# Row sums of the first triangle stage on ScalarE, low parts of two batches made one stage later, and a new order of words

## The chip, the cores and the metric

The kernel runs on one core of a Trainium2 chip. The metric is the device time of one execution in microseconds (us). Before the change three runs took 3619.18, 3623.9 and 3624.72 us; the median is 3623.9.

## What is computed

The input is x, four batches of 64 x 64 positions with 256 channels, in float32. Two layers follow each other. The first is an attention over the 4096 positions of a batch with 32 channels for its factors f and g:

```
f = xt @ Wf + bf;  g = xt @ Wg + bg;  v = xt @ Wh + bh
beta = softmax(einsum('bqd,bkd->bqk', g, f))
x = x + (einsum('bqk,bkd->bqd', beta, v) @ Wo + bo)
```

The second is a triangle attention over the 64 x 64 positions with 8 heads, layer norms and an MLP:

```
scores = einsum('bilhd,bljhd->biljh', q, k) / sqrt(32)
att = softmax(scores, axis=2)                       # over l
out = einsum('biljh,bilhd,bljhd->bijhd', att, v1, v2)
h = layer_norm(x_in + out @ Wo)
x = layer_norm(relu(h @ W1 + b1) @ W2 + b2 + h)
```

The change touches the softmax sums over l of the triangle attention of batch 0, and the factors f and g of the attention of batches 2 and 3.

## The kernel before, in words

A batch goes through a token stage (`layer0`, the first attention and the projections of the second layer) and a triangle stage (`first_layer1` for batch 0, `next_layer1` for the others). Token stages and triangle stages follow each other; all that batch 0's triangle stage has to spare is used to make the inputs of batches 1, 2 and 3. Each engine works its own queue in order, and all queues are filled in the order of the program.

**The triangle stage.** It has 32 steps: four pairs of heads by eight groups of eight rows i (`NIG`, `IG`). What a step needs is made in pieces that words name:

- `sp`, `sf`: the score matmuls for a pair (L940), into a tile of the PSUM pool psA, which has two buffers and also holds the accumulators; `e`, `f`: ScalarE's exponentials of them into the SBUF tile S (L950).
- `S`: for one step, VectorE sums the 8 rows of 64 exponentials into `dens` (L967) and takes the reciprocal (L969). `W`: ScalarE multiplies each row by its reciprocal (L977). `t`: TensorE turns the result into the PSUM tile att (L994). `c`: ScalarE copies the last two or three of its eight pieces to the SBUF tile attP (L1002)[...].
- `R`: one of the eight products of a step with v2, 128 x 2048 float32 (L1042). The last `npool(step)` of the eight are made by GpSimd from attP into tile Rp (two buffers), the others by VectorE from att into tile R (three buffers). In batch 0 `npool` is 3, and 2 in every fourth step.
- `V`: ScalarE writes the stationary weights wsel from v1 (L1021). `A`: TensorE accumulates one product (L1052). `T`: ScalarE takes one of the two accumulators of a step to SBUF (L1062), and after the second the step's eight stores go out on SP's queue (L1071).

In the triangle stage of batch 0 other words stand between these. For piece s (512 tokens; pieces 0 to 7 are batch 1, 8 to 15 batch 2, 16 to 23 batch 3), class `Ahead` makes the inputs of a later token stage: `v` the value matmuls from tile xT (L383), `u` their copy out (L390); `g` the matmuls of g and f into a PSUM tile of the pool psB (L251), `a` ScalarE's copy of them with bias, rounded to the number format of the score matmuls, the high part (L260), `b` VectorE's low part, the sum with bias less the high part (L265), and the store of both to DRAM (L273). A copy of the high and low parts is spread later to the tiles gT and fT by DMAs on GpSimd's queue (L278, L284). When both `v` and `g` of piece s are done, the load of the xT of piece s + 2 is issued on SP's queue (L377). The words `m`, `n`, `o`, `p` are projections of batch 0 that are left over from its token stage (L481, L443).

**The order.** `ORDER0` is a list of words that is gone through once for each of 11 periods. A period is four steps; the word `R25/2` stands for product 5 of step 4i + 2, and the number after the slash is i's lag: i is the period less 2. A word whose step or piece doesn't exist does nothing; words of step 0 for `S`, `W`, `V`, `t` and `c` do nothing either, since `layer0` has done them. Periods with i from 0 to 3 handle two pieces s each, and periods with i from 4 to 7 four.

**The token stage.** `layer0` runs over g = 0 to 63, eight groups for each of eight query blocks. For each g, TensorE makes four score matmuls (L563) and four value matmuls (L590), ScalarE two exponentials (L575), VectorE an addition to the running sum (L597). After each group a piece of the query block before is done (`parts`): the normalisation, the output and the projections, whose results go to DRAM on SP's queue. Nothing of `Ahead` is in the token stage of batch 1.

Of the kernel before, what the change touches and what calls it, by code (L numbers as in the profile page):

```python
# [25 lines left out]
IG = 8  # L26
NIG = N // IG
# [37 lines left out]


ORDER0 = """
    A21/2 g1/2 S3/1 W1/1 A27/2 A23/2 A26/2 a1/2 V3/2 A24/2 R32/2 b1/2 m1/2 T20/2 c3/2 t0/1 v2/2 n1/2 R25/2 A25/2
    R33/2 sp0/1 T21/2 A32/2 R34/2 R36/2 R30/2 A33/2 e00/1 u2/2 e01/1 o1/2 R31/2 g2/2 c0/1 R37/2 A34/2 A36/2
    A30/2 A31/2 A37/2 V0/1 R35/2 T30/2 t1/1 R00/1 p1/2 a2/2 b2/2 A35/2 R03/1 T31/2 sf0/1 A00/1 R02/1 g0/1 f0/1  # L70
    a0/1 b0/1 R05/1 f1/1 R07/1 A05/1 A03/1 v3/2 R06/1 u3/2 m0/1 S2/1 W2/1 c1/1 v0/1 V1/1 R01/1 A02/1 n0/1 R04/1
    A07/1 A01/1 A04/1 R12/1 u0/1 A06/1 T00/1 sp1/1 T01/1 R13/1 R15/1 R14/1 A13/1 e10/1 e11/1 t2/1 R10/1 A12/1
    R17/1 V2/1 A15/1 A14/1 A10/1 R16/1 R11/1 S0 R22/1 W3/1 g3/2 c2/1 W0 A17/1 R27/1 A11/1 v1/1 R20/1 a3/2 b3/2
    u1/1 o0/1 p0/1 S1 R21/1 T10/1 t3/1 A16/1 T11/1 A20/1 R23/1 A22/1 R24/1 R26/1
""".split()


@with_exitstack
def attention_then_triangle_kernel(
# [174 lines left out]
                    )  # L254


    def biased(ps, t):
        ps = ps.rearrange("p (w t) -> p w t", w=4)
        for w, bias in enumerate((bias_g, bias_f)):
            nc.scalar.activation(t[:, 0, w, :].bitcast(PART), ps[:, w, :], AF.Identity, bias=bias)  # L260

    def parted(ps, t):
        ps = ps.rearrange("p (w t) -> p w t", w=4)
# [5 lines left out]
    def parts_tile(**where):  # L269
        return work.tile([P, 2, 2, P], F32, name="gf", **where)  # L270

    def store_parts(d, q, t, queue):
        queue.dma_start(out=d[q], in_=t)  # L273
# [68 lines left out]
    class Ahead:  # L342
        def __init__(self):
            shapes = {"x": [C, T], "v": [P, NKC, P], "gf": [8, P, 2, 2, P]}
            self.d = {
                b: {n: dram.tile(sh, F32, tag="ah" + n, name="ah" + n, bufs=NB) for n, sh in shapes.items()}
                for b in range(1, NB)
            }
            self.n = 8 * (NB - 1)
            self.raw, self.xT, self.vp, self.gf, self.t = {}, {}, {}, {}, {}  # L350
            self.parts = None

        def bring(self, s):
# [43 lines left out]
        def factored(self, s):  # L397
            if self.parts is None:
                self.parts = work.tile([P, 2, 2, 2, P], F32, tag="hid", name="gf", bufs=1)
            self.t[s] = self.parts[:, s % 2]  # L400
            biased(self.gf[s], self.t[s])

        def parted(self, s):
            t = self.t.pop(s)
            parted(self.gf.pop(s), t)
            store_parts(self.d[1 + s // 8]["gf"], s % 8, t, nc.sync)


# [99 lines left out]
    def layer0(b, F, safe, rest, ahead):  # L508
# [257 lines left out]
        for g in range(8 * NQB):  # L766
            qb, k = divmod(g, 8)
            if b == 0 and not safe:
                for load in later[3 * g : 3 * g + 3]:
                    load()  # L770
                if g == 6:
                    fold_bias()
                if g == 20:
                    add_b2()
            if safe and k == 0 and qb + 1 < NQB:
                mx, todo = pieces(qb + 1)
                for qc, t in todo:
                    max_piece(qc, t, mx)
                row[qb + 1] = max_row(mx)
            values(g, g + 1 < 8 * NQB)  # L780

            if qb > 0 and not (qb == last and k >= 6 + late):
                for part in parts[k]:
                    part(qb - 1)
            if late and g % 2 == 0 and 0 <= g // 2 - 2 < ahead.n:
                ahead.bring(g // 2 - 2)
            if late and g % 2 == 1 and 0 <= g // 2 - 3 < ahead.n:
                ahead.turn(g // 2 - 3)
            for do, after in (
                (rest.recall, -3), (rest.settle, 0), (rest.rooted, 1), (rest.polished, 2), (rest.scaled, 3), (rest.finish, 4),  # L790
            ):
                if b > 1 and g - after in SETTLED:
                    do(NP * (b - 2) + SETTLED.index(g - after))
            if g == 1 and b > 0 and not safe:
                limits(b - 1)
            if qb == last and k == 3:
                L.fetch_v1(0)
                L.fetch_v1(1)
            if qb == last and k == 5:
                if b > 0:  # L800
                    rest.load(NP * (b - 1))
                L.fetch_qk(0, True)
# [81 lines left out]
    class Layer1:  # L884
        def __init__(self, b, io, safe):
            self.b, self.io, self.safe = b, io, safe

            self.aT = dram.tile([C, 2, N // 2, N], F32, tag="aT", name="aT")
            io["a"] = self.aT
            self.S, self.v2, self.qk, self.v1, self.att, self.ao = {}, {}, {}, {}, {}, {}  # L890
            self.R, self.begun, self.acc, self.rec, self.e = {}, {}, {}, {}, {}
            self.owed = lambda: None

# [57 lines left out]
                )  # L953


        def sums(self, step):
            pair, ig = divmod(step, NIG)
            rows = self.S[pair][:, ts(ig, IG), :]
            if self.safe:
                nmx = small.tile([P, IG], F32, tag="mxl", name="mxl")  # L960
                nc.vector.tensor_reduce(nmx, rows, AX.X, ALU.max, negate=True)
                den = small.tile([P, IG], F32, tag="den", name="den")
                for i in range(IG):
                    nc.scalar.activation(rows[:, i, :], rows[:, i, :], AF.Exp, bias=nmx[:, i : i + 1])
            else:
                den = dens[:, ts(step, IG)]
            nc.vector.tensor_reduce(den, rows, AX.X, ALU.add)  # L967
            rec = small.tile([P, IG], F32, tag="rd", name="rd")
            nc.vector.reciprocal(rec, den)  # L969
            self.rec[step] = (rows, rec)  # L970
# [8 lines left out]

        def npool(self, step):  # L980
            if self.b == 0:
                return 2 if step % 4 == 3 else 3
            return 3 - step % 2


# [431 lines left out]
    def step_words(L, fetched, stored, spread, late=None):  # L1417
        made, taken, sps = {}, {}, {}

        def do(w, step, m):  # L1420
            if not 0 <= step < NSTEP:
                return
            if w == "R":
                if step not in made:
                    made[step] = 0
                    L.begin(step)
                L.product(step, m)
                made[step] += 1
                if made[step] == 4:
                    spread(step)  # L1430
                if made[step] == 8:
                    if step == 1:
                        L.fetch_v2(1)
                    if step == NIG - 1 and late is not None:
                        L.fetch_v2(2, 2)
                        late.room = True
                        late.fetch()
                    elif step in (NIG - 1, 2 * NIG - 1):
                        L.fetch_v2((step + 1) // NIG + 1)
                    fetched(step + 1)  # L1440
            elif w == "A":
                L.accumulate(step, m)
            elif w == "T":
                L.take(step, m)
                taken[step] = taken.get(step, 0) + 1
                if taken[step] == 2:
                    L.store(step)
                    stored(step)
            elif step == 0:
                return  # L1450
            elif w == "S":
                L.sums(step)
            elif w == "W":
                L.weights(step)
            elif w == "V":
                L.stationary(step)
                L.fetch_v1(step + 2)
            elif w == "t":
                L.turn_weights(step)
            elif w == "c":  # L1460
                L.copy_weights(step)


        def scores(j):
            if 0 <= j < 12:
                L.scores(1 + j // 4, j % 4)
                sps[j] = L.sp
                if j % 4 == 3 and j // 4 + 2 < NPAIR:
                    L.fetch_qk(j // 4 + 2)

        def take_scores(j, half):
            if 0 <= j < 12:
                L.sp = sps[j]
                L.take_scores(half)

        L.fetch_v1(2)
        return do, scores, take_scores
# [6 lines left out]
    def first_layer1(L, ahead, F):  # L1484
# [29 lines left out]
        for period in range(NSTEP // 4 + 3):  # L1514
            if period == 1:
                L.owed()
            for word, late in words_of(ORDER0):
# [10 lines left out]
                elif word[0] == "f":  # L1528
                    if i == 0:
                        take_scores(0, last)  # L1530
                elif word[0] in "RATSWVtc":
                    step_word(word[0], 4 * i + int(word[1]), last)
                elif word[0] in "mnop":
                    if 0 <= i < 4:
# [199 lines left out]
```

## Time and profile before

One execution was profiled. It took 3623.49 us; the span of the program in it is 3621.6 us, at a mean granted TensorE clock of 0.993.

| | us |
|---|---|
| median of three runs | 3623.9 |
| profiled execution, and its span | 3623.49, 3621.6 |
| TensorE busy over the span | 3516.2 |
| VectorE | 2849.8 |
| ScalarE | 1923.5 |
| GpSimd | 1777.1 |
| first triangle stage, first product to the end of the last | 443.5 to 868.2 |
| first score matmul of the second token stage | 872.2 |

Busy time is the union of an engine's instructions. Matmuls are pipelined and their ends modelled, so a busy TensorE needn't be at its peak. L12 is line 12 of the kernel; PE is TensorE's matmuls, PEld its weight loads, DVE VectorE, ACT ScalarE, POOL GpSimd, SP the queue of most DMAs. The idle time before an instruction is put down to what released it last.

### The profile page before, as it was taken

To read this page: it belongs to the slowest core of one execution; us is meant where nothing else is said; L and a number is where in the kernel's file an instruction comes from. 1 tells how busy PE (TensorE), PEld (TensorE's weight loads), DVE (VectorE), ACT (ScalarE), POOL (GpSimd) and SP (SyncE) were. 2 spreads that over 40 slices of the span, in tenths; PEclk is the share of its full clock that TensorE was granted. 3 is DMA by queue.
4 is the path that set the end of the run, shared out by engine and by line. 5 is a ranking of instruction groups with operands and counts; after the bars stand their busy time and mean duration, and the time that the engine had idled before them with its cause. 6 is when DMAs were issued, how large, how long until landed. Compare 5 with 4: busy or idle time off the path is not lost.

```text
span 3621.6 us, 58681 instructions
## 1 busy us (share of the span) xinstructions
PE 3516.2 (97%) x22218; PEld 1887.8 (52%) x22218; DVE 2849.8 (79%) x2662; ACT 1923.5 (53%) x4221; POOL 1777.1 (49%) x904
## 2 busy tenths in 40 slices
PE   9999999988999999999999999999999999999998
PEld 6555444434555555554455555555355555555477
DVE  4777499996555569999777749999787766999987
ACT  3444455544444366665444446666444446777655
POOL 5000099995000058899111118989611116999920
PEclk9999999999999999999999999999999999999999
DMA  9444555456111264426322254343633335441221
GB/s 174 137 132 125 138 151 133 126 132 139 47 50 50 81 153 102 108 62 114 96 95 88 82 141 117 83 104 79 131 93 99 96 108 142 96 94 49 66 69 57
DMA packets 509492, 374.37 MB, mean 103 GB/s; under 512 B 320080, under 2 KB 450896, under 8 KB 500368
## 3 DMA queue, kind: packets, MB, share of 16 engines
q1 hardware_dynamic: 460160, 343.56, 34.7%
q0 software_dynamic: 36160, 19.94, 5.5%
q10 hardware_dynamic: 12880, 7.01, 0.7%
q8 instruction: 178, 2.92, 0.3%
q14 instruction: 114, 0.93, 0.1%
HBM read 205.73 MB, written 164.63 MB: 102 GB/s over the span
## 4 chain that ended last, share of the span: by engine, by line
PE 68%; POOL 7%; DVE 6%; issue 4%; ACT 2%; DMA 0%; SPq 0%; ACTq 0%; DVEq 0%; POOLq 0%
PE o L590 18%; PE acc L1052 17%; PE proj L673 6%; POOL Rp L1042 6%; PE s L563 5%; PE mp L1303 5%; PE zp L1323 5%; PE sp L940 3%; DVE R L1042 3%; PE v1p L705 2%; PE hp L1160 2%; PE y L642 1%; PE att L994 1%; PE htp L1270 1%; PE hp L1166 0%
## 5 line engine op out<-in xcount | busy, mean ns | idle before, releaser
L1042 POOL TENSOR_TENSOR Rp<-attP,v 128x2048 f32<-128x2048 f32 x328 | 1491.3, 4579 | 410.4 <-ACT attP L1002 367.3
L1042 DVE TENSOR_TENSOR R<-att,v 128x2048 f32<-128x2048 f32 x696 | 1545.9, 2277 | 70.4 <-PE acc L1052 51.8
L590 PE MATMUL o<-e,v 128*128 128x512 f32 x2048 | 1043.7, 592 | 0.0
L575 ACT ACTIVATE e<-s 128x1024 f32<-128x1024 f32 x512 | 522.9, 1023 | 532.4 <-PE s L563 447.6
L597 DVE TENSOR_TENSOR esum<-esum,e 128x2048 f32<-128x2048 f32 x224 | 511.8, 2285 | 369.9 <-ACT e L575 367.9
L563 PE MATMUL s<-gT,fT 128*128 128x512 f32 x1024 | 786.5, 770 | 8.8 <-ACT e L575 4.7
L1052 PE MATMUL acc<-R,wsel 128*32 128x512 f32 x5568 | 705.4, 602 | 27.7 <-DVE R L1042 20.4
L590 PEld LDWEIGHTS o<-e,v 128*128 128x128 f32 x2048 | 388.3, 190 | 276.7 <-issue 233.8
L1062 ACT COPY ao<-acc 128x1024 f32<-128x1024 f32 x256 | 256.3, 1012 | 291.5 <-PE acc L1052 203.3
L1052 PE MATMUL acc<-Rp,wsel 128*32 128x512 f32 x2624 | 345.5, 598 | 22.3 <-POOL Rp L1042 21.6
L1052 PEld LDWEIGHTS acc<-R,wsel 128*32 128x32 f32 x5568 | 155.4, 110 | 397.6 <-issue 277.4
L1337 POOL TENSOR_TENSOR hz<-hz,log_bc 128x512 f32<-128x512 f32 x32 | 45.6, 1426 | 599.9 <-ACT hz L1247 599.9
L563 PEld LDWEIGHTS s<-gT,fT 128*128 128x128 f32 x1024 | 194.4, 190 | 245.0 <-issue 231.9
L977 ACT ACTIVATE es<-S,rd 128x64 f32<-128x64 f32 x1024 | 258.3, 337 | 15.0 <-DVE rd L969 13.1
L1231 POOL TENSOR_SCALAR nt<-mv 128x2 f32<-128x2 f32 (+1 forms) x49 | 9.4, 191 | 505.1 <-DVE mv L1186 500.0
L1303 PE MATMUL mp<-hT,w 128*128 128x256 f32 x1024 | 244.7, 384 | 1.7 <-ACT hT L1275 1.7
L1323 PE MATMUL zp<-w,hid 128*128 128x256 f32 x1024 | 240.0, 385 | 2.5 <-ACT hid L1312 2.1
L1323 PEld LDWEIGHTS zp<-w,hid 128*128 128x128 f32 x1024 | 187.9, 190 | 50.1 <-issue 14.7
L1303 PEld LDWEIGHTS mp<-hT,w 128*128 128x128 f32 x1024 | 185.2, 190 | 54.7 <-ACT attP L1002 12.6
L619 DVE RECIPROCAL rec<-den 128x512 f32<-128x512 f32 x32 | 107.4, 3357 | 126.5 <-PE den L615 121.2
L1052 PEld LDWEIGHTS acc<-Rp,wsel 128*32 128x32 f32 x2624 | 80.9, 110 | 210.1 <-issue 143.6
L950 ACT ACTIVATE S<-sp 128x512 f32<-128x512 f32 x128 | 131.4, 1092 | 77.9 <-PE sp L940 77.9
(195 smaller groups left out, 3699.0 us busy)
## 6 DMA issues: line engine op xcount, KB each, us to landing
v<-v2d SPq DMA_DIRECT2D x44, 512.0 KB
v1c<-v1d SPq DMA_DIRECT2D x128, 128.0 KB
aT<-ao SPq DMA_DIRECT2D x1024, 16.0 KB
A<-aT SPq DMA_DIRECT2D x256, 64.0 KB
hz<-raw SPq DMA_DIRECT2D x32, 512.0 KB
y<-yT SPq DMA_DIRECT2D x56, 256.0 KB
q<-st SPq DMA_DIRECT2D x56, 256.0 KB
k<-st SPq DMA_DIRECT2D x52, 256.0 KB
```

The source lines that it names most:

```text
L563: nc.tensor.matmul(s_ps[r // 2][:, r % 2, :], fT[tt][:, ts(r * 4 + n, P)], gT[qb // 4][:, ts(qb % 4, QB)], start=True, stop=not safe,)
L575: nc.scalar.activation(e[g][:, 2 * j : 2 * j + 2, :], s_ps[j], AF.Exp)
L590: nc.tensor.matmul(o_ps[qb], F.v[tt][:, r * 4 + n, :], es[:, r, :], start=(k == 0 and r == 0), stop=(k == 7 and r == 3),)
L597: nc.vector.tensor_tensor(esum[qb], esum[qb], es, ALU.add)
L673: nc.tensor.matmul(ps, w[:, cc, rows], y(qb, cc), start=(cc == 0), stop=(cc == 1))
L950: nc.scalar.activation(self.S[pair][:, :, l0 : l0 + 8].rearrange("p i l -> p l i"), sp[:, lh], AF.Copy if self.safe else AF.Exp,)
L977: nc.scalar.mul(e[:, i, :], rows[:, i, :], rec[:, i : i + 1])
L1042: eng.tensor_tensor(R, src.unsqueeze(1).to_broadcast([P, D, N]), v2[h], ALU.mult)
L1052: nc.tensor.matmul(acc[32 * c : 32 * c + 32, n % 2, :], w[:, n, c, 16 * h : 16 * h + 32], R[:, ts(c, 8), :].rearrange("p d j -> p (d j)"), ...
L1062: nc.scalar.copy(self.ao[step][:, ts(np, 2)].rearrange("p k d j -> p k (d j)"), self.acc[step][np])
L1303: nc.tensor.matmul(self.mp[:, fc % 2, :], w1_sb[:, cc, ts(fc, P)], self.hT[tt][:, cc, :], start=(cc == 0), stop=(cc == 1),)
L1323: nc.tensor.matmul(zp[:, n, :], self.hid[tt][:, fc, ts(n, P)], w2_sb[:, fc, :], start=(fc == 0), stop=(fc == 3 and tt not in self.hT2),)
```

## The change

1. A new word `K` for each step of the first triangle stage. `row_sums` has ScalarE pass over each of the step's 8 rows with Identity, writing the row onto itself, and take the sum of the row into `dens` with the accumulator output. `sums` then leaves out VectorE's reduce for that step and keeps the reciprocal. Step 0 is summed by VectorE as before.
2. For pieces 8 to 23 (batches 2 and 3) `biased` writes g and f with bias unrounded, and `parted` issues only the store of that, half as large. In the second token stage, `bring_whole` loads such a piece back (for g = 10, 13, ... 55), and two to three rounds later (g = 15, 18, ... 60) `part` has ScalarE make the rounded high part and VectorE the low part, and stores both. The tile has the tag s4, of which there are two buffers. Pieces 0 to 7 stay as they were.
3. `npool` in batch 0 is read from a list of 32 digits, `ON_POOL`; they sum to 83.
4. `ORDER0` is a new list. Its lags differ too: no word has the lag 0 any more, and products 1, 3, 5 and 7 of step 4i + 1 and all of step 4i + 2 have the lag 2.

```diff
 ORDER0 = """
...
+    S3/2 A14/2 R17/2 t2/2 e11/2 o0/2 A12/2 b0/2 K0/1 c2/2 V2/2 R13/2 v2/2 R11/2 R15/2 A17/2 R27/2 W3/2 S0/1
+    A10/2 A13/2 R22/2 R23/2 u2/2 p0/2 A15/2 A11/2 v1/2 T10/2 A22/2 T11/2 A27/2 A23/2 t3/2 m1/2 R21/2 u1/2 R26/2
+    A21/2 R24/2 g1/2 A26/2 A24/2 K1/1 g2/2 c3/2 W0/1 R20/2 A20/2 R25/2 A25/2 n1/2 t0/1 o1/2 a1/2 a2/2 T20/2
+    R32/2 b2/2 v3/2 V3/2 A32/2 V0/1 R37/2 T21/2 A37/2 R35/2 R36/2 R30/2 p1/2 A30/2 c0/1 R34/2 u3/2 A35/2 v0/1
+    A34/2 R31/2 A36/2 K2/1 R33/2 R05/1 sf0/1 T31/2 A31/2 u0/1 R07/1 A33/2 b1/2 S1/1 sp0/1 R04/1 g3/2 T30/2 W1/1
+    e01/1 A05/1 R06/1 A04/1 R03/1 R01/1 e00/1 t1/1 V1/1 f0/1 m0/1 c1/1 A07/1 f1/1 A01/1 K3/1 R00/1 S2/1 A03/1
+    R02/1 g0/1 A06/1 R14/1 A00/1 A02/1 W2/1 R12/1 R10/1 T01/1 a0/1 sp1/1 T00/1 a3/2 R16/1 n0/1 A16/1 b3/2 e10/1
 """.split()
+
+ON_POOL = "23323323233233323233323223322332"
...
-    def biased(ps, t):
+    def biased(ps, t, whole=False):
         ps = ps.rearrange("p (w t) -> p w t", w=4)
         for w, bias in enumerate((bias_g, bias_f)):
-            nc.scalar.activation(t[:, 0, w, :].bitcast(PART), ps[:, w, :], AF.Identity, bias=bias)
+            o = t[:, 0, w, :]
+            nc.scalar.activation(o if whole else o.bitcast(PART), ps[:, w, :], AF.Identity, bias=bias)
...
-            biased(self.gf[s], self.t[s])
+            biased(self.gf[s], self.t[s], whole=s >= 8)
...
         def parted(self, s):
-            t = self.t.pop(s)
-            parted(self.gf.pop(s), t)
+            t, gf, d = self.t.pop(s), self.gf.pop(s), self.d[1 + s // 8]["gf"]
+            if s < 8:
+                parted(gf, t)
+                store_parts(d, s % 8, t, nc.sync)
+            else:
+                nc.sync.dma_start(out=d[s % 8][:, 0], in_=t[:, 0])
+
+        def bring_whole(self, s):
+            t = self.whole[s] = parts_tile(tag="s4")
+            nc.sync.dma_start(out=t[:, 1], in_=self.d[1 + s // 8]["gf"][s % 8][:, 0])
+
+        def part(self, s):
+            t = self.whole.pop(s)
+            nc.scalar.activation(t[:, 0].bitcast(PART), t[:, 1], AF.Identity)
+            nc.vector.tensor_tensor(t[:, 1].bitcast(PART), t[:, 1], t[:, 0], ALU.subtract)
             store_parts(self.d[1 + s // 8]["gf"], s % 8, t, nc.sync)
...
+            if b == 1 and g % 3 == 1 and 8 <= g // 3 + 5 < ahead.n:
+                ahead.bring_whole(g // 3 + 5)
+            if b == 1 and g % 3 == 0 and 8 <= g // 3 + 3 < ahead.n:
+                ahead.part(g // 3 + 3)
...
+        def row_sums(self, step):
+            pair, ig = divmod(step, NIG)
+            if not self.safe:
+                for i in range(IG):
+                    row = self.S[pair][:, ig * IG + i, :]
+                    nc.scalar.activation(
+                        row, row, AF.Identity, accum_out=dens[:, step * IG + i : step * IG + i + 1]
+                    )
+                self.summed.add(step)
...
-            nc.vector.tensor_reduce(den, rows, AX.X, ALU.add)
+            if step not in self.summed:
+                nc.vector.tensor_reduce(den, rows, AX.X, ALU.add)
...
             if self.b == 0:
-                return 2 if step % 4 == 3 else 3
+                return int(ON_POOL[step])
```

More of the change, by code (lines that the diff above doesn't have):

```diff
@@ L67 @@
 ORDER0 = """
[L68 to L74, printed above, removed]
+    S3/2 A14/2 R17/2 t2/2 e11/2 o0/2 A12/2 b0/2 K0/1 c2/2 V2/2 R13/2 v2/2 R11/2 R15/2 A17/2 R27/2 W3/2 S0/1
[5 more added lines that the diff above has]
+    R02/1 g0/1 A06/1 R14/1 A00/1 A02/1 W2/1 R12/1 R10/1 T01/1 a0/1 sp1/1 T00/1 a3/2 R16/1 n0/1 A16/1 b3/2 e10/1
 """.split()
+ON_POOL = "23323323233233323323233223322332"
 @with_exitstack
@@ L349, in __init__ @@
             self.n = 8 * (NB - 1)
-            self.raw, self.xT, self.vp, self.gf, self.t = {}, {}, {}, {}, {}
+            self.raw, self.xT, self.vp, self.gf, self.t, self.whole = {}, {}, {}, {}, {}, {}
             self.parts = None
@@ L892, in __init__ @@
             self.owed = lambda: None
+            self.summed = set()
         def fetch_qk(self, pair, first=False):
@@ L1450, in do @@
                 return
+            elif w == "K":
+                L.row_sums(step)
             elif w == "S":
@@ L1530, in first_layer1 @@
                         take_scores(0, last)
-                elif word[0] in "RATSWVtc":
+                elif word[0] in "RATKSWVtc":
                     step_word(word[0], 4 * i + int(word[1]), last)
```

## Prediction

> **What bounds the kernel now.** I first looked for the stretch that the change touches. The busy table by slices of the page shows GpSimd full in the slices from about 440 to 870 us; the timeline puts the first product (L1042) of the first triangle stage at 443.5 us and the last one's end at 868.2, and the next stage's first score at 872.2. Then I asked for the busy time of each engine in stretches (start:end, length, and busy us of PE, PEld, DVE, ACT, POOL, then clock, DMA share, GB/s):
>
> ```profile
> 443.50:868.20 424.70, 382.74 (x4196) 176.12 (x4196) 404.44 (x270) 219.07 (x577) 408.23 (x102) 0.97 0.56 138
> 500.00:550.00 50.00, 47.59 (x531) 22.43 (x533) 49.16 (x33) 27.90 (x73) 48.71 (x12) 1.00 0.55 140
> 800.00:850.00 50.00, 39.98 (x368) 17.64 (x364) 40.05 (x27) 18.48 (x48) 45.50 (x16) 0.86 0.85 177
> 873.00:1250.00 377.00, 375.19 (x1047) 197.56 (x1046) 201.85 (x136) 158.38 (x178) 0.00 (x0) 1.00 0.17 58
> ```
>
> In the triangle stage VectorE is busy 98% of an ordinary stretch and GpSimd 97%; ScalarE is half empty. In the second token stage TensorE is busy throughout, VectorE and ScalarE about half. The groups of VectorE in the stage say what fills it (count, then busy us, mean ns, idle us ahead and its releasers):
>
> ```profile
> L1042 DVE TENSOR_TENSOR R<-att,v 128x2048 f32<-128x2048 f32 x168 | 373.0, 2274 | 18.0 <-PE acc L1052 11.5 <-ACT attP L1002 3.5 <-DMA k<-k 2.9
> L967 DVE TENSOR_REDUCE dens<-S 128x8 f32<-128x512 f32 x29 | 19.6, 674 | 0.0
> L265 DVE SCALAR_TENSOR_TENSOR gf<-gf,bias_g 128x128 fp32r<-128x128 f32 x22 | 7.5, 342 | 4.2 <-ACT gf L260 3.9
> L265 DVE SCALAR_TENSOR_TENSOR gf<-gf,bias_f 128x128 fp32r<-128x128 f32 x22 | 7.5, 341 | 0.0
> L969 DVE RECIPROCAL rd<-dens 128x8 f32<-128x8 f32 x29 | 5.9, 203 | 1.0
> ```
>
> Its idle is 424.7 - 404.4 = 20.3 us. One third is a single hole, seen in three timelines (start, us, engine): a load of xT issued late, the vp matmul that waits for it with the later accumulations queued behind it on TensorE, and VectorE out of buffers for 6.58 us.
>
> ```profile
> 837.37 1.94 SPq L377 DMA_DIRECT2D xT<-ahx  x2
> 843.10 1.24 PE L383 MATMUL vp<-wh,xT 128*128 128x128 f32 x3 [4.53 <-DMA xT<-ahx]
> 849.99 2.29 DVE L1042 TENSOR_TENSOR R<-att,v 128x2048 f32<-128x2048 f32 x1 [6.58 <-PE acc L1052]
> ```
>
> **What the skill says.** "Perfetto Trace Analysis", Identifying the Most-Contended Engine: occupancy is fair for VectorE and GpSimd but not for matmuls. The trace agrees: PE shows 382.7 us busy, but by start-to-start distances its stage needs less (below). "ScalarE: Activation LUTs", What ACT_TABLE_LOAD costs: an ACTIVATE costs 186 ns + 0.833 ns an element, 93 ns more for each pointer operand, and neighbours overlap by 93 ns. The trace agrees: 64 elements with a pointer scale (L977) take 340 ns (by the rule 332). "GPSIMD Engine Reference", Specifications: GpSimd shares SBUF interfaces with VectorE when the latter has two SBUF inputs. Here a VectorE product reads att from PSUM, so moving products should not alter their prices; no run here shows the other case.
>
> **The change part by part.**
>
> *Row sums.* Of 31 reduces of steps 1 to 31, 29 lie in the stretch (two ran ahead of it, in idle time). A reduce costs VectorE 0.70 us from its start to the reciprocal's (the timeline has 557.47 and 558.17): -29 x 0.70 = -20.3 us. The two reciprocals that come into the stretch add 2 x 0.12. ScalarE gets 31 x 8 = 248 ACTIVATEs of 64 elements, each with an accumulator read. The nearest pair in the trace is this (second triangle stage):
>
> ```profile
> 1409.77 0.39 ACT L1201 ACTIVATE junk<-hp 128x256 f32<-128x256 f32 x1
> 1410.05 0.20 ACT L1201 ACTIVATION_READ_ACCUMULATOR junk<-hp 128x1 f32 x1
> 1410.14 0.38 ACT L1201 ACTIVATE junk<-hp 128x256 f32<-128x256 f32 x1
> ```
>
> A pair takes 0.37 us at 256 elements; 192 fewer at the skill's 0.833 ns are -0.16, so an estimate of 0.21. The highest bound is 0.34 + 0.20 = 0.54 without overlap; the floor is the ACTIVATE alone by the same rule, 0.24 less 0.09 of overlap, 0.15. I take 0.25, a little above the pair: 62 us over the stage, 7.8 per period of four steps. ScalarE then holds 219 + 62 = 281 of some 415 us. It covers them with its own idle time; without that cover they would cost up to 62 us.
>
> *Low parts.* Two L265 operations take 0.52 us from start to the next start. 14 of the 16 pieces concerned lie inside the stretch (24 pieces, 22 shown): -14 x 0.52 = -7.3 us. The L273 store shrinks from both parts to one, so SP's queue has as many issues as before.
>
> *Products.* The digits of the new list sum to 83 for GpSimd, before 8 x 2 + 24 x 3 = 88. So VectorE gets 5 more, at 373.0/168 = 2.22 us: +11.1. GpSimd loses 5 x 4.58 = 22.9 us and stops being co-bound (408 - 23 = 385).
>
> VectorE inside the stage: -20.3 + 0.2 - 7.3 + 11.1 = **-16.3 us**.
>
> *Start.* Step 1's sum was ready before the first product. Now K1 comes behind the copies of step 0 on ScalarE (which end at 444.4), takes 2.0 us and S1, ahead of the first VectorE product in the new order, waits for it: start 446.6 instead of 443.5, **+3.1 us**. Queued behind S1 are all VectorE products; GpSimd's first three go on.
>
> *Order, the hole.* On the old list the load follows g3, and v1, which needs it, comes with no VectorE product between them. On the new list the shortest such distance, g1 to v3, holds R20, R32 on VectorE and R25 on GpSimd, over 4.4 us, and SP has its eight L1071 stores elsewhere. From issue to use it took 843.10 - 837.37 = 5.7 us here, so the hole mostly closes: **-6.6**, at worst 0.
>
> *Order, TensorE.* From start-to-start distances: an accumulate 0.86 (256), a group of transposes 0.5 (32), scores 1.9 (12), vp 1.9 (24), gf 0.87 (24), v2p 1.8 (8), v1p 1.9 (8): 355 us, 44.4 per period. VectorE's period was 21 x 2.22 + 4 x 0.82 + 2.75 x 0.52 = 51.3 and becomes 21.6 x 2.22 + 4 x 0.12 + 0.52 = 49.0. TensorE's margin shrinks from 6.9 to 4.6. VectorE's idle apart from the hole and two start gaps (2.2 + 2.0) is 20.3 - 6.6 - 4.2 = 9.5 us; an order that I can't price from the trace could give less or double it. I scale it by 6.9/4.6: 14.3, **+4.8** (bounds -9.5 and +9.5).
>
> *Waits added.* S waits for K. Behind S on VectorE stand the next products; but three to five products (6.6 us and more) lie between K and S in the list from step 2 on, against K's 2.0 us: nothing. Behind K on ScalarE stand attP copies and takes; 7.8 us a period is in its idle.
>
> *Second token stage.* 16 pieces get a load and a store on SP (128 and 256 KB), one ScalarE pass over 256 elements (0.4) and one VectorE subtraction (0.42, as L1403). A load is issued five score groups, about 28 us, ahead of its use. Tile s4 has two buffers, so a load stands on SP behind the store two pieces back; y and projection stores queue behind it for a few us. ScalarE and VectorE have idle of 0.5 us and more per us, so TensorE covers nearly all. A subtraction at the end of a query block can push the reciprocal, and y after it, by 0.4 in two of seven blocks: **+1** (0 to 2; if SP's wait reached the projections, more).
>
> Sum: -16.3 + 3.1 - 6.6 + 4.8 + 1 = **-14.0**. The profiled execution took 3623.49 us (span 3621.6 and 1.9 around it), the median of the runs is 3623.9: so 3609.5, for the median 3609.9; I give 3610.
>
> **Rivals.**
> A, the order is simply better: no added idle and a few us of the old 9.5 less: -16.3 + 3.1 - 6.6 - 1 + 1 = -19.8, so 3604; down to 3597. For it: GpSimd's 23 us of slack. Against: TensorE's margin.
> B, given back: TensorE, in order and at 90% load, becomes the bound; waits of accumulations for takes (eight of 1.7 us before, by the table of waits) multiply to five us a period: 44.4 + 5 = 49.4, the hole stays, idle doubles: -16.3 + 3.1 + 9.5 + 1 = -2.7, so 3621.
> C, slower: a row on ScalarE costs its two durations and a wait for its own write back, 0.65 us. ScalarE's period is 219/8 = 27.4, and its forced waits ahead of takes some 9.4 (1.2 each, eight); with 31 rows: 36.8 + 20.2 = 57 against 424.7/8 = 53.1 before: 8 x 3.9 = +31, so 3655. It decides from (53.1 - 36.8)/31 = 0.53 us a row. Against it: the pair above.
>
> **Numbers.** Main case 0.56 (own range 3602 to 3617), A 0.18, B 0.14, C 0.12. A measurement of this kernel tells 0.2%, about 7 us, from no change: the line is at 3616.7. Faster: nearly all of main and A, 0.71; same: B and the main's edge, 0.16; slower: C and a little of B, 0.13. Range 3597 to 3626; C is left out, with the far tail of A.
>
> **What would show it.** L967 x1 in the stage and its row sums as pairs near 0.25 us; VectorE's first product near 446.6; no wait of vp for xT over 3 us; VectorE near 97% busy in ordinary stretches and the stage's last product near 853; the second token stage as long as before. It is wrong if ScalarE is over 90% busy in the stage, if VectorE's idle exceeds 30 us, or if TensorE waits in the second token stage.

## The result, and the profile after

The changed kernel took 3606.56 us (median of six runs, 3604.37 to 3607.5); six runs of the kernel before, three of them new, have the median 3620.32. The ratio is 0.996, with a 95% interval from 0.9949 to 0.9972, so the change gains 0.4%, 13.8 us between the two medians. The profiled execution took 3607.5 us, the longest of the six, with a span of 3605.3. The forecast was 3610, faster. Of the 16.3 us between the two spans, 16.05 had been won when the second token stage began: its first score matmul comes at 856.17 us instead of 872.22. From there to the first product of the second triangle stage it is 427.6 us in both.

The busy table of the changed kernel shows the stretches of the prediction and two more (start:end, length, busy us of PE, PEld, DVE, ACT, POOL, clock, DMA share, GB/s). The first line runs from the first product to the end of the last.

```profile
443.00:854.30 411.30, 379.27 (x4209) 176.69 (x4208) 388.82 (x220) 277.73 (x1076) 386.80 (x98) 0.98 0.57 139
500.00:550.00 50.00, 43.85 (x493) 20.64 (x490) 42.79 (x25) 34.85 (x136) 41.04 (x10) 0.93 0.55 140
550.00:600.00 50.00, 49.90 (x551) 24.23 (x552) 50.00 (x31) 36.32 (x138) 48.97 (x12) 1.00 0.54 134
600.00:650.00 50.00, 44.18 (x484) 19.64 (x483) 42.67 (x28) 31.96 (x116) 43.89 (x10) 0.93 0.58 142
800.00:850.00 50.00, 44.28 (x472) 19.20 (x468) 49.61 (x27) 23.83 (x76) 49.98 (x17) 1.00 0.76 173
873.00:1250.00 377.00, 375.77 (x1053) 198.53 (x1053) 208.14 (x150) 159.70 (x190) 0.00 (x0) 1.00 0.22 70
```

The stage is 411.3 us long instead of 424.7. VectorE's busy time fell by 15.6 us, ScalarE's rose by 58.7, and GpSimd's fell by 21.4. The stretch with the old hole, 800 to 850, is now full. But the stretch from 500 to 550, which was full, has 7 us of idle on VectorE and 9 on GpSimd, and the one from 600 to 650 has 7 and 6. The groups of the stage, VectorE's and then ScalarE's (count, busy us, mean ns, idle us ahead and its releasers):

```profile
L1078 DVE TENSOR_TENSOR R<-att,v 128x2048 f32<-128x2048 f32 x173 | 383.4, 2275 | 26.2 <-PE acc L1088 20.2 <-ACT attP L1038 4.5 <-ACT es L1013 0.9
L1005 DVE RECIPROCAL rd<-dens 128x8 f32<-128x8 f32 x31 | 5.9, 191 | 0.7 <-ACT S L986 0.7
L270 DVE SCALAR_TENSOR_TENSOR gf<-gf,bias_f 128x128 fp32r<-128x128 f32 x8 | 2.7, 340 | 0.0
```

```profile
L986 ACT ACTIVATE S<-S 128x64 f32<-128x64 f32 x248 | 59.7, 245 | 0.5
L986 ACT ACTIVATION_READ_ACCUMULATOR S<-S 128x1 f32 x248 | 47.1, 190 | 0.0
L517 ACT COPY sx<-v1p 128x512 f32<-128x512 f32 x8 | 4.7, 588 | 21.0 <-DMA v2d<-sx 21.0
```

The reduces are gone from VectorE, 8 pairs of low parts are left, and 173 products cost what they cost before. The last line is new: before, the copies into tile sx waited 1.0 us in all; now ScalarE stands 21.0 us in front of the copies of v1p, in five waits for the store of the tile's last content. Two of them are long, 8.7 and 8.6 us. In the order of time the timeline of the changed kernel has (start, us, engine; in brackets the idle ahead):

```profile
517.24 9.84 SPq L1107 DMA_DIRECT2D aT<-ao  x8
527.17 0.53 SPq L510 DMA_DIRECT2D v2d<-sx  x1
530.26 0.59 ACT L517 COPY sx<-v1p 128x512 f32<-128x512 f32 x1 [8.74 <-DMA v2d<-sx]
531.82 1.94 PE L1088 MATMUL acc<-R,wsel 128*32 128x512 f32 x8 [6.15 <-ACT ao L1098]
533.82 2.29 DVE L1078 TENSOR_TENSOR R<-att,v 128x2048 f32<-128x2048 f32 x1 [5.28 <-PE acc L1088]
```

Eight stores, which take SP 5.0 to 6.9 us in most places of this stage, take 9.84 behind the loads of q and k for the next pair; the store of sx comes behind them. Tile sx has one buffer, so ScalarE's next copy into it waits 8.74 us; behind that copy stand the takes of the accumulators, TensorE waits for these, and VectorE runs out of buffers. The same chain comes again near 634 us. With the small gaps that follow, the two cost VectorE 6.8 and 7.3 us.

The slow stores themselves are not new. In the kernel before, SP's timeline has

```profile
510.96 0.37 SPq L491 DMA_DIRECT2D v2d<-sx  x1
517.96 10.98 SPq L1071 DMA_DIRECT2D aT<-ao  x8
```

There the store of sx went out before the loads of q and k; the new order puts it behind them. What makes the stores slow is that SP waits for those loads among them. For 514 to 531 us the changed kernel's table of SP's waits (us in total, times, longest) has

```profile
SPq L1107 <- DMA k<-k: 3.6, 2, 1.9
SPq L1107 <- DMA q<-q: 1.3, 1, 1.3
```

That is 4.9 us, all that 9.84 has above 5. At the second place it is 5.5 of 10.51, and in the kernel before 6.3 of 10.98.

Part of each stall comes after the wait. Between 531 and 535 us, right after TensorE's wait of 6.15 us, its granted clock was 0.50, and the eight accumulations at 531.82 took 1.94 us; at 535.20, with the clock near 1 again, eight took 1.03.

### The profile page after: what moved, and what is told of

Read it like the earlier page. It is cut to its first block, busy times and chain, and to the rows that moved or that the text cites. A ratio compares the mean times of both kernels' runs of the same rounds, so it can differ in the third digit from the quotient of the medians.

```text
span 3605.3 us, 59250 instructions
## 1 busy us (share of the span) xinstructions
PE 3506.9 (97%) x22218; PEld 1885.3 (52%) x22218; DVE 2837.0 (79%) x2620; ACT 1987.7 (55%) x4733; POOL 1755.3 (49%) x899
## 4 chain that ended last, share of the span: by engine, by line
PE 80%; POOL 7%; DVE 4%; issue 4%; DMA 2%; ACT 2%; SPq 0%; ACTq 0%; POOLq 0%; DVEq 0%
PE o L609 24%; PE acc L1088 19%; PE proj L692 8%; PE s L582 7%; POOL Rp L1078 5%; PE zp L1359 4%; PE mp L1339 4%; PE sp L964 3%; PE v1p L724 2%; PE hp L1196 2%; PE y L661 2%; PE att L1030 1%; DVE R L1078 1%; PE v1p L462 1%; PE vp L388 1%
## 5 line engine op out<-in xcount | busy, mean ns | idle before, releaser
L1078 POOL TENSOR_TENSOR Rp<-attP,v 128x2048 f32<-128x2048 f32 x323 | 1469.4, 4581 | 419.1 <-DMA k<-k 305.4
L1088 PE MATMUL acc<-R,wsel 128*32 128x512 f32 x5608 | 704.8, 598 | 23.4 <-ACT ao L1098 11.2
L1088 PE MATMUL acc<-Rp,wsel 128*32 128x512 f32 x2584 | 339.9, 598 | 24.5 <-POOL Rp L1078 22.9
L1088 PEld LDWEIGHTS acc<-R,wsel 128*32 128x32 f32 x5608 | 158.6, 109 | 384.9 <-issue 278.2
L1339 PEld LDWEIGHTS mp<-hT,w 128*128 128x128 f32 x1024 | 185.1, 190 | 55.1 <-ACT hid L1348 13.4
```

The source lines that it names most:

```text
L1078: eng.tensor_tensor(R, src.unsqueeze(1).to_broadcast([P, D, N]), v2[h], ALU.mult)
L1088: nc.tensor.matmul(acc[32 * c : 32 * c + 32, n % 2, :], w[:, n, c, 16 * h : 16 * h + 32], R[:, ts(c, 8), :].rearrange("p d j -> p (d j)"), ...
L1339: nc.tensor.matmul(self.mp[:, fc % 2, :], w1_sb[:, cc, ts(fc, P)], self.hT[tt][:, cc, :], start=(cc == 0), stop=(cc == 1),)
```

## The experiments

Each ratio below is to runs of the kernel before made beside those of the kernel; the medians of these lie between 3620.3 and 3622.7 us, so ratios are to be compared, not medians. A ratio has an interval of about 0.0012 to each side, so two differ safely from some 0.0016, 6 us. The stage is measured in one profiled execution, from the first product on either engine to the end of the last, since the moment of the first product differs by some 4 us between the profiled executions. The idle is that length less VectorE's busy time.

| kernel | median us | ratio to before | stage us | VectorE busy, idle | GpSimd busy | ScalarE busy |
|---|---|---|---|---|---|---|
| before | 3620.3 | 1 | 424.7 | 404.4, 20.3 | 408.2 | 219.1 |
| changed | 3606.6 | 0.996 | 411.3 | 388.8, 22.4 | 386.8 | 277.7 |
| e1_two_sx | 3603.2 | 0.995 | 411.2 | 388.1, 23.1 | 387.3 | 278.1 |
| e2_sums_dve | 3618.5 | 0.9992 | 421.1 | 409.3, 11.8 | 387.6 | 218.6 |
| e3_parts_back | 3619.5 | 0.9993 | 419.1 | 395.7, 23.4 | 387.5 | 278.2 |
| e4_order_alone | 3626.1 | 1.0012 | 424.5 | 405.5, 19.1 | 408.8 | 218.9 |
| e5_digits_old | 3619.3 | 0.9994 | 421.5 | 379.8, 41.7 | 408.7 | 278.6 |
| e6_qk_on_act | 3608.2 | 0.9965 | 412.6 | 388.6, 23.9 | 387.7 | 278.0 |
| e7_qk_on_act_two_sx | 3604.3 | 0.9958 | 407.6 | 388.1, 19.5 | 386.7 | 277.9 |
| e8_sums_alone | 3628.1 | 1.0023 | 429.0 | 385.6, 43.4 | 407.9 | 277.4 |
| e9_low_alone | 3622.7 | 0.9999 | 421.9 | 397.4, 24.5 | 408.2 | 219.1 |
| e10_sums_twice | 3612.7 | 0.9975 | 418.5 | 389.1, 29.5 | 387.2 | 334.6 |
| e11_two_sx_two_yb | 3597.7 | 0.9936 | 401.8 | 388.4, 13.4 | 386.7 | 277.6 |
| e12_sums_digits | 3667.5 | 1.0132 | 461.4 | 398.0, 63.5 | 385.4 | 277.2 |

### One part of the change taken back

**e2_sums_dve**: VectorE makes the row sums again.

```diff
             elif w == "K":
-                L.row_sums(step)
+                pass
```

> The changed kernel with word K doing nothing, so that VectorE makes the row sums again; order, digits and low parts as changed. Theory (VectorE sets the stage's end): 31 reduces of 0.70 us come back, +21.7 us less what falls into the two gaps of the sx tile, some 18 to 22, ratio 1.001 to 1.002. Rival (the gaps come from a busier ScalarE): the gaps shrink as ScalarE loses its 60 us, and the time rises by under 10 us, 0.9985.

The ratio is 0.0032 above the changed kernel's, 11.6 us. It lies between the two theories. VectorE's busy time rose by the 20.4 us that were expected, but its idle fell from 22.4 to 11.8: with ScalarE less busy, the gap at the start (0.65 and 3.12 us) falls to 0.26 and the first gaps of the two sx stalls fall from 5.28 and 4.91 to 3.00 and 3.06. So ScalarE's idle hid the sums only in part: about half of what they take off VectorE comes back as waits.

**e3_parts_back**: all low parts in the triangle stage.

```diff
-            biased(self.gf[s], self.t[s], whole=s >= 8)
+            biased(self.gf[s], self.t[s])
...
-            if s < 8:
+            if True:
                 parted(gf, t)
...
-            if b == 1 and g % 3 == 1 and 8 <= g // 3 + 5 < ahead.n:
+            if False and g % 3 == 1 and 8 <= g // 3 + 5 < ahead.n:
...
-            if b == 1 and g % 3 == 0 and 8 <= g // 3 + 3 < ahead.n:
+            if False and g % 3 == 0 and 8 <= g // 3 + 3 < ahead.n:
```

> The changed kernel with all low parts made by VectorE in the triangle stage and none in the second token stage. Theory: 16 pairs of 0.52 us come back on VectorE, +7 to +8 us, ratio 0.998; the second token stage is as long as before, since what it lost was hidden. Rival (GpSimd and TensorE are as late as VectorE): +0 to +2 us, 0.9962.

The time rose by 0.0033, 12 us, more than either theory has. The stage is 7.8 us longer, as expected. The rest isn't in the stage: from its first score to the next triangle stage's first product, the token stage took 427.6 us in every other kernel with these parts moved or with the old list, but 435.1 here and 434.1 in e4_order_alone. (The profiled execution of e3_parts_back, 3623.85 us, is the longest of its thirteen; the medians leave only some 4 us beside the 7.8.) The timeline of e3_parts_back at the handover from the triangle stage to the token stage shows why:

```profile
864.79 1.21 PE L582 MATMUL s<-gT,fT 128*128 128x512 f32 x4
...
869.64 0.37 ACT L265 ACTIVATE gf<-gf,bias_g 128x128 fp32r<-128x128 f32 x1 [4.58 <-DMA ahgf<-gf]
869.91 0.36 ACT L265 ACTIVATE gf<-gf,bias_f 128x128 fp32r<-128x128 f32 x1
870.16 1.94 ACT L594 ACTIVATE e<-s 128x1024 f32<-128x1024 f32 x2
...
871.23 0.79 PE L582 MATMUL s<-gT,fT 128*128 128x512 f32 x1 [5.23 <-ACT e L594]
```

ScalarE's copy of the last piece waits for the store of a low and high part that is late, since VectorE made its low part behind its last product (862.78 us). The exponentials of the token stage stand behind that copy. In the changed kernel the store of the unrounded g and f waits for no VectorE work, and the copy (at 856.48) waits for nothing.

**e5_digits_old**: `npool` as before, 88 products on GpSimd.

```diff
-                return int(ON_POOL[step])
+                return 2 if step % 4 == 3 else 3
```

> The changed kernel with npool as before (88 products on GpSimd instead of 83). Theory (GpSimd and VectorE are balanced at 83): VectorE loses 11 us of work, GpSimd gains 23 and is busy some 409 us of a stage that ended after 411, so the time rises by 4 to 10 us, ratio 0.9975 to 0.999. Rival (VectorE alone sets the end): the time falls by about 8 us, 0.9935.

It is 0.0034 slower, 12.3 us, somewhat above the theory's range; the rival falls. VectorE has 9.0 us less to do and 19.3 more idle, while GpSimd is busy 408.7 us of a 421.5 us stage. Not all of it is GpSimd's load: the first digit is 3 here, so all that VectorE makes of step 0 stands behind S1, and its first product comes at 446.91 us, 3.2 us after GpSimd's.

So each of the three parts, taken back alone, takes nearly the whole gain with it (0.9992, 0.9993 and 0.9994). Their costs, 11.6, 12 and 12.3 us, can't be added up to a gain of 14.

### One part alone, on the kernel before

**e4_order_alone** has the new list with the words K doing nothing, the old digits and the low parts in the triangle stage (the edits of e2, e3 and e5 together).

> The new list of words alone on the kernel before: no row sums on ScalarE, low parts in the triangle stage, npool as before. Theory: the hole of 6.6 us at the load of xT and 2 us at the stage's tail go, the two sx gaps of 6 to 7 us come, so the time moves by -2 to +6 us, ratio 1.000 to 1.002. Rival (the order is what brought the gain): -10 us or more, 0.997.

The ratio is 1.0012 (1.0005 to 1.0018), inside the theory's range; the new list alone brings nothing. The stage is as long as before: the hole is gone, but the stalls near 530 and 635 us are there, if smaller (first gaps 2.98 and 2.65), with ScalarE waiting 24.7 us in all for the store v2d<-sx. So the order makes these waits, without the row sums. 6.5 us are lost in the token stage behind.

**e8_sums_alone** has the old list with four words put in, all else as before.

```diff
 # in ORDER0 of before, each in front of the word named
+ K2/1    # a0/1
+ K0      # t2/1
+ K1      # W0
+ K3      # T11/1
```

> The kernel before with the row sums on ScalarE alone: the old list with the words K0, K1, K2, K3 put in ahead of t2, W0, a0 and T11; digits and low parts as before. Theory (GpSimd, busy 408 us with 88 products, is next behind VectorE, and ScalarE's 45 us come in front of copies that others wait for): a gain of 2 to 8 us, ratio 0.998 to 0.9995. Rival (VectorE alone bounds, and ScalarE's idle hides the sums whatever the order): -17 to -20 us, 0.995.

It is slower than before, 1.0023 (1.0013 to 1.0033): outside both. VectorE lost 18.9 us of work and gained 23.1 of idle, and the stage is 4.3 us longer. GpSimd's timeline says where the period of four steps comes from (the first line is of the kernel before, the others of e8_sums_alone):

```profile
526.01 49.96 POOL L1042 TENSOR_TENSOR Rp<-attP,v 128x2048 f32<-128x2048 f32 x11 [1.29 <-ACT attP L1002]
537.25 49.96 POOL L1078 TENSOR_TENSOR Rp<-attP,v 128x2048 f32<-128x2048 f32 x11 [1.15 <-PE acc L1088]
588.32 13.66 POOL L1078 TENSOR_TENSOR Rp<-attP,v 128x2048 f32<-128x2048 f32 x3 [1.11 <-PE acc L1088]
```

Eleven products and a short wait make 588.32 - 537.25 = 51.07 us. In the kernel before it is the same eleven, and 577.24 - 526.01 = 51.23. GpSimd was as much the bound as VectorE, and relief for VectorE alone is worth nothing. The loss in the stage is at its start, where the first reciprocals now wait 7.46 and 1.71 us for ScalarE and VectorE's first product comes at 445.04 us, 5.1 after GpSimd's.

**e9_low_alone** is the kernel before with the low parts moved (the change's edits to `biased`, `parted`, `bring_whole`, `part` and `layer0`, and no others).

> The kernel before with the low parts of batches 2 and 3 moved to the second token stage, nothing else (old list, old digits, row sums on VectorE). Theory (GpSimd with 88 products is as late as VectorE, and the old list has no stall at the handover to the token stage): VectorE loses 7 to 8 us of work, but the period stays near 51 us, a gain of 1 to 4 us, ratio 0.999 to 1.000. Rival (the move is worth what it was worth on the new list): -13 us, 0.9965.

The ratio is 0.9999 (0.9991 to 1.0007): no difference from before, and inside the theory's range; the rival falls. The profiled stage is 2.8 us shorter, though the runs don't show it.

**e12_sums_digits** is e8_sums_alone with the digits of `ON_POOL`.

> The kernel before with the row sums on ScalarE (old list with K words) and the new digits; low parts in the triangle stage. Theory (GpSimd bounded the run with the sums alone): with 83 products on GpSimd VectorE sets a period of 49.9 us against 51.1, so 8 to 10 us less than the sums alone, ratio 0.9995. Rival (the old list itself holds the period): no less than the sums alone, 1.002.

The theory falls. The rival is right that it is no faster than the sums alone, but its size is far off: it is 1.3% slower than before. GpSimd has 22 us less to do than in e8_sums_alone, yet stands far more. The table of waits in the stage has

```profile
POOL Rp L1078 <- PE acc L1088: 65.5, 12, 14.2
...
DVE R L1078 <- PE acc L1088: 42.1, 24, 6.3
```

(us in total, times, longest). TensorE accumulates in the order of the list. The likely reading is that with other digits this order no longer fits the order in which the two engines finish, so that products wait in their buffers for a turn behind one that isn't made yet; the waits agree with it, but no run tests it on its own. The lesson is that list and digits belong together: new digits on the old list lost here, old digits on the new list in e5_digits_old.

### The cover on ScalarE

**e10_sums_twice** makes each row sum twice.

```diff
                 L.row_sums(step)
+                L.row_sums(step)
```

> The changed kernel with every row summed twice on ScalarE (the second pass gives the same sums), which adds another 60 us to ScalarE and nothing to VectorE. Theory (ScalarE's idle covers the sums only in part, since takes and copies stand behind them): +6 to +14 us, ratio 0.998 to 1.000. Rival (the prediction's: ScalarE, then busy 82% of the stage, hides them): +0 to +3 us, 0.9965.

The ratio rose by 0.0015, 5.4 us, which two ratios can hardly tell apart, and it lies between the rival's range and the theory's. But the stage is 7.2 us longer with VectorE's busy time the same. That speaks for the theory in kind, at its lower edge, and agrees with e2_sums_dve: ScalarE has room (it is busy 80% of the stage), and still each us put on it costs some 0.1 us here; what stands behind it in the queue comes later.

### The two stalls

**e1_two_sx** gives tile sx two buffers.

```diff
-                st = work.tile([P, 512], F32, tag="sx", name="sx", bufs=1)
+                st = work.tile([P, 512], F32, tag="sx", name="sx", bufs=2)
```

The tile junk of a later stage shares the tag and gets the same edit.

> The changed kernel with two buffers of tile sx in place of one, nothing else. Theory (one buffer): the two gaps of 8.7 and 8.6 us in which ScalarE waits at the copy sx<-v1p for the store v2d<-sx go, and with them VectorE's two gaps of 6 to 7 us each near 529 and 633 us; VectorE's idle in the stage falls from 22.5 to about 10, and the time by about 12 us, to a ratio of 0.9927 to before. Rival (TensorE's smaller margin makes the idle, as the prediction had it): the gaps move elsewhere and the time stays, 0.996.

The theory falls: the ratio, 0.995 (0.9936 to 0.9963), can't be told from the changed kernel's. ScalarE's waits for the store are gone, but VectorE's idle is not: 23.1 us. The first stall is shorter (4.71 us), and the second took another way, as the timeline and the table of waits of this kernel show.

```profile
641.00 2.29 DVE L1078 TENSOR_TENSOR R<-att,v 128x2048 f32<-128x2048 f32 x1 [8.49 <-ACT sx L509]
```

```profile
PEld v2p L500 <- DMA yb<-y: 13.3, 6, 6.8
ACT sx L509 <- PE v2p L500: 11.3, 2, 8.1
```

The load of tile yb, also with one buffer, stands on SP's queue behind the same stores. TensorE now waits for it, ScalarE for TensorE.

**e6_qk_on_act** and **e7_qk_on_act_two_sx** move the loads of q and k to ScalarE's queue, the second with two sx buffers.

```diff
-        def fetch_qk(self, pair, first=False):
+        def fetch_qk(self, pair, first=False, queue=nc.sync):
...
-                nc.sync.dma_start(
+                queue.dma_start(
...
-                if j % 4 == 3 and j // 4 + 2 < NPAIR:
+                if late is None and j % 4 == 3 and j // 4 + 2 < NPAIR:
                     L.fetch_qk(j // 4 + 2)
...
                 L.take_scores(half)
+                if late is not None and half == 1 and j % 4 == 3 and j // 4 + 2 < NPAIR:
+                    L.fetch_qk(j // 4 + 2, queue=nc.scalar)
```

> The changed kernel with the two loads of q and k for pairs 2 and 3 issued from ScalarE's queue after the last exponential of the pair, in place of SP's queue; one sx buffer. Theory (SP's queue is held for 10 us by the eight stores of ao behind those loads, and the store of sx stands behind them): the stores take 5 to 6 us again, ScalarE's waits of 8.7 and 8.6 us at sx shrink to under 3, VectorE's idle in the stage falls by some 10 us, ratio 0.9935. Rival (the stores are slow because the transfers themselves are slow, whoever issues the loads): the gaps stay, 0.996.

> The same with two sx buffers as well. Theory: with SP's queue free the second buffer adds little, at most 3 us more than with one buffer, ratio 0.9925 to 0.9935. Rival (the transfers are slow whoever issues them): as with two sx buffers alone, 0.995.

Neither brought what the theory expected, and the times are the rivals'. The rival's reason, slow transfers whoever issues the loads, is not shown, though. In e6_qk_on_act the first eight stores took 5.90 us, as the theory had it, but the wait moved to ScalarE, whose loads of k now waited in its own queue for a store of ao:

```profile
521.93 0.26 ACT L986 ACTIVATE S<-S 128x64 f32<-128x64 f32 x1 [7.30 <-DMA aT<-ao]
```

The second eight took 8.21, and a copy into sx still waited 9.0 us. In e7_qk_on_act_two_sx, with the loads of q and k gone from SP, the first eight stores took even longer:

```profile
511.17 14.55 SPq L1107 DMA_DIRECT2D aT<-ao  x8
```

3.5 us of that are a wait for ScalarE; 5.6 and 3.1 us are waits for transfers of q and of ao. The Trainium skill says in "DMA: Bandwidth & Descriptors", Issuing engines are not separate DMA queues, that DMAs started by different engines run on the same 16 DMA engines. Nothing in these two runs contradicts that: with another issuing engine the wait changed its place and did not go.

**e11_two_sx_two_yb** takes both dependences away: the copies of v2p and of v1p get a tile each in place of the one sx, and yb gets a second pair of tiles and is loaded one piece earlier.

```diff
-            self.load(0)
+            self.ys, self.used = {}, {}
+            for q in range(2):
+                self.load(q)
...
-            self.y = []
-            for cc, tag, bufs in ((0, "A", 1), (1, "yc", 1)):
+            self.ys[q] = []
+            for cc, tag, bufs in ((0, ("A", "st")[q % 2], (1, 3)[q % 2]), (1, "yc", 2)):
...
-            if self.used == 2 and q + 1 < NQB:
-                self.load(q + 1)
+            if self.used[q] == 2 and q + 2 < NQB:
+                self.load(q + 2)
...
-                st = work.tile([P, 512], F32, tag="sx", name="sx", bufs=1)
+                st = work.tile([P, 512], F32, tag="sx" if w == "n" else "h", name="sx", bufs=1)
...
```

> The changed kernel with a second sx buffer and a second pair of yb buffers, so that yb is loaded one piece earlier. Theory (with two sx buffers the wait moved to the load of yb, which stands on SP's queue behind the same slow stores): the waits for sx and yb go both, VectorE's idle in the stage falls to some 12 us, ratio 0.993 to 0.994. Rival (the next thing on SP's queue, the stores of ao and the loads of v1c, takes over): as with two sx buffers, 0.995.

The theory holds: idle 13.4 us, stage 401.8, ratio 0.9936 (0.9922 to 0.9949). Its median, 3597.7 us, is the lowest of all the kernels. The eight stores behind the loads of q and k still take 9.69 and 10.33 us, so the slow stores stay and only what hung on them is gone: the stalls of the changed kernel came from single buffers refilled behind slow stores, and were worth 9.5 us of the stage.

## Why the prediction was right, and where it was not

The mechanism was right in the main: the gain is VectorE's work in the first triangle stage, kept by moving products off GpSimd too. By its own steps:

- **VectorE's work**, -16.3: measured -15.6. The price of a row on ScalarE, 0.25 us, measured 0.24 (lines in the last section); ScalarE's busy time, 281, measured 277.7. Rival C needed 0.53 a row and falls with it.
- **Start**, +3.1: wrong, about 0. The step took all of R05, R06 and R07 of step 0 for GpSimd. The first digit is 2, so R05 is VectorE's and stands ahead of S1 in the list. The first product came at 443.0 and the wait for K1 was 0.65 us; the two start gaps together are 3.8 us, before 4.2. The chain itself was right: in e5_digits_old, where the first digit is 3, VectorE's first product came at 446.91, for which the step had 446.6.
- **The hole**, -6.6: right. The longest wait of vp for xT is 0.8 us.
- **TensorE's margin**, +4.8: wrong in kind. Idle beyond hole and start rose from 9.5 to 18.6 us, by 9.1, nearly twice the term and just inside its upper bound, but 14.2 of the 18.6 are the two sx stalls and only 4.4 the rest, less than before. e11_two_sx_two_yb shows it: TensorE has the same work there, and the whole idle falls to 13.4. What the prediction missed is that on the new list the store of sx stands behind the loads of q and k and the eight stores, which were as slow in the trace of before, while sx has one buffer.
- **The cover of ScalarE**, nothing: wrong in part. e2_sums_dve and e10_sums_twice agree that putting work on it costs time behind it; by e2_sums_dve the row sums gain 11.6 us net, where 20 us of VectorE's work had gone.
- **Low parts**, -7.3 in the stage: right there (e3_parts_back: 7.8). The store that no longer waits for VectorE at the handover wasn't seen: another 7.5 us in the profiled execution of e3_parts_back, on the new list only.
- **The handover**, no term: the last product's end to the first score fell from 4.0 to 1.9 us. That is the list's doing, since e4_order_alone has 1.9 and e9_low_alone 4.0: on the old list 16 matmuls of vp (2.05 us) came last, behind the accumulations.
- **GpSimd**, "stops being co-bound": right, and more needed than it said. e5_digits_old and e8_sums_alone show that without the digits there is little or no gain.
- **Second token stage**, +1: nothing measured, its lower bound.

The measured sum of the stage is -15.6 - 0.4 - 6.6 + 9.1 = -13.5, and -2.1 at the handover. So the sum was near in part by luck: two errors, the start and the missed handover, lay on one side and the missed stalls on the other. Rival A's time, 3604, was as near to the measured median, but only because six runs put the kernel before 3.6 us lower than three had. As a gain, the two medians have 13.8 us with an interval from 10 to 18.5, where the likeliest case had 14.0 and A 19.8. A's mechanism, no added idle, was not what happened either: e11_two_sx_two_yb is nearer to that.

What stays open: why SP waits for the loads of q and k in the middle of stores that need nothing of them. The new digits alone, and the new list with the new digits alone, were not run. And e9_low_alone and e10_sums_twice are too near to their neighbours for the runs alone to tell.

## What to carry to other kernels

Where two engines are equally full, relief for one can show nothing until the other is relieved as well and the order is made to fit: here the row sums alone, the low parts alone and the order alone changed the time by +0.2%, 0 and +0.1%, and all of it together by -0.4%. When an order is new, look at each tile with one buffer and at each queue that its refill stands on, since a store that was early enough by chance no longer is. Idle on an engine with an in-order queue isn't free cover: ask what stands behind the new work.

## What the runs showed of the hardware that was not expected

In the changed kernel's stage, eight stores of ao held SP's queue for 5.0 to 6.9 us in most places, for 9.84 and 10.51 us behind the loads of q and k (10.98 and 10.46 in the kernel before), and for 11.31 and 11.47 behind loads of v. Of these 4.9, 5.5, 6.6 and 5.4 us are SP's waits for the loads. With the loads of q and k issued from ScalarE the stores took 5.90 and 8.21 us in one kernel and 14.55 and 8.49 in the other.

An ACTIVATE over 64 elements with a read of its accumulator takes ScalarE 0.24 us from row to row, though the two instructions last 0.245 and 0.190 us on average:

```profile
444.14 0.24 ACT L986 ACTIVATE S<-S 128x64 f32<-128x64 f32 x1
444.28 0.19 ACT L986 ACTIVATION_READ_ACCUMULATOR S<-S 128x1 f32 x1
444.38 0.24 ACT L986 ACTIVATE S<-S 128x64 f32<-128x64 f32 x1
```

The read starts 0.14 us after its ACTIVATE, before that has ended, and the next row starts 0.10 us after the read.
